# Counts in bf16 beside fp32 sums, biases in three bf16 parts, and ten register loads made one, in a one-core graph kernel

## The chip, the cores and the metric

The kernel runs on one core of a Trainium2 chip. The core has a matrix engine (PE, with its weight loads shown apart as PEld), a vector engine (DVE), an activation engine (ACT), GpSimd (POOL) and a queue engine for transfers (SP), each with an instruction stream of its own; semaphores tie them together. The metric is the device time of one execution in microseconds (us), as the median of several runs. One further execution was profiled, and the rows shown come from it.

## The reference

12,500 nodes with 128 features, 400,000 edges sorted by destination, each of one of two kinds. Cut to what matters:

```python
Xs = X[src]
m_data = Xs @ W_data.T + b_data
m_ctrl = Xs @ W_control.T + b_control
msg = jnp.where((edge_types == 0)[:, None], m_data, m_ctrl)
agg = jax.ops.segment_sum(msg, dst, num_segments=N)
h = relu(agg + (X @ W_self.T + b_self))
out = layernorm(X + h)            # no scale or shift
```

Since the sum is linear, the kernel sums the raw rows of `X` per destination and kind first, and multiplies by the weights once per node. The two edge biases then enter as a number of edges times a bias: a node with 20 edges of the first kind and 12 of the second gets 20 b_data + 12 b_control. That is what the counts are for.

## The kernel before, in words

**Groups and windows.** The edges are cut into 25 groups of 125 chunks of 128 edges; one group covers 500 destinations. In a group there are five windows, and in each window two kinds of work. In the first, whole rows of `x` (in three bf16 parts that add up to fp32) are gathered by indirect transfers on POOL (`msg`), a comparison on DVE makes a 0/1 matrix (`psel`) of which edge goes to which destination, and PE multiplies the two (L738). In the second, the rows are picked out of a copy of `x` held on the chip: DVE makes matrices `pick` and `esel`, PE picks rows (`got`, L893), ACT copies them to `emsg` (L907), and PE adds them up with `esel` (L738 again). A long chain of small DVE operations (`O`, `prod`, `found`, `rank`, `rm`, `rv`, `key`, `top`) works out where an edge goes, for a later pair of windows.

**Sums and counts.** Each window's sums land in PSUM (`sums`). `accumulate` (L782) adds them on DVE into `acc[g]`, an fp32 tile of 128 partitions by 3 planes by 640 destinations: planes 0 and 1 hold the sums for the two kinds, plane 2 the counts, kept in partitions 0 and 32 (a matmul with a matrix whose first column is ones, L824, makes them). A fixed 1 in partition 2 stands for the node's own bias. Where a window lies in the 640 columns is known only at run time: `place_of` (L776) reads that column number out of a small tile `place_i` into a DVE register, ten times in most groups (232 times in all), just ahead of the `accumulate` that uses it. Each read is three instructions on DVE's instruction stream: a TENSOR_LOAD, a FUSED_REGOPS and a SEQ_ASSERT that holds the value to its range. Every `accumulate` has one more FUSED_REGOPS, which makes the addresses.

**End of a group.** `pass_on` (L766) adds the last 140 columns of a group's `acc` to the next group's. `finish` then makes the output in four tiles of 125 nodes: per tile the fp32 matmuls of L1012 are x by W_self, the two planes of sums by their weights, and plane 2 by a matrix `bias` that has the three biases in rows 0, 32 and 2. Each fp32 matmul stands in the trace as two passes. Then come relu, the residual, the normalization and the store. `begin_acc` (L750) fills a new `acc` by a transfer from a stored start value.

**Order.** The program is written out in full, without loops at run time. The kernel's code gives a rough order by time fractions, and a scheduler then places the instructions on each engine; on DVE and on the other engines they run in that order. The register reads are kept behind an earlier `accumulate`. A second, slow path (`long_path`) runs only if one of the checks (`check_all`) finds that the edges don't fit the layout.

Of the kernel before, what the change touches and what calls it, by code (L numbers as in the profile page):

```python
# [8 lines left out]
FP = mybir.dt.float32  # L9
BF = mybir.dt.bfloat16  # L10
# [3 lines left out]
AF = mybir.ActivationFunctionType  # L14
OP = mybir.AluOpType
AX = mybir.AxisListType
# [3 lines left out]
P = 128  # L20
D = 128
# [4 lines left out]
NG = NC // GC  # L26
GN = P * GC * N // E
# [20 lines left out]
OVF = 64  # L48
TOP = 7
HOLD = 18  # L50
AHEAD = 14
# [154 lines left out]
def short_path(ctx, tc, const, ident, eps, wT, brow, bad, x, src, dst, etype, ws, bs, out):  # L206
    nc = tc.nc
# [32 lines left out]
    raw = {}  # L240
# [76 lines left out]
    tmp = early.enter_context(tc.tile_pool(name="tmp", bufs=1))  # L317
    wn = tmp.tile([P, 3, D], FP, name="wn")
    bias = keep.tile([P, D], FP, name="bias")
    nc.gpsimd.memset(bias, 0.0)  # L320
# [33 lines left out]


    start1 = keep.tile([P, 1], FP, name="start1")
    nc.vector.tensor_single_scalar(start1, lane_f, 2.0, op=OP.is_equal)
# [20 lines left out]
    nc.vector.memset(one_col[:, 0:1], 1.0)  # L378

    worst = keep.tile([P, 5, P], FP, name="worst")  # L380
    nc.vector.memset(worst, 0.0)
# [13 lines left out]
    def places_and_weights():  # L395
        place = tmp.tile([1, 2, NG, NWIN], FP, name="place")
        ref = tmp.tile([1, NG, NE, 2], I32, name="ref")
        nc.gpsimd.iota(ref, pattern=[[GN, NG], [0, NE], [-PAD, 2]], base=PAD - M0, channel_multiplier=0)
        ref = ref.rearrange("o g e k -> o g (e k)")
        for at, k in enumerate("pe"):  # L400
                each = place[:, 0].rearrange("o g (i k) -> o g i k", k=2)[:, :, :, at]
                nc.vector.tensor_tensor(
                    each, first_i[k], ref.rearrange("o g (i k) -> o g i k", k=2)[:, :, :, at], op=OP.subtract
                )
        nc.vector.tensor_tensor(place[:, 1], place[:, 0], least, op=OP.max)
        nc.vector.tensor_scalar(place[:, 1], place[:, 1], float(R - WMAX), None, op0=OP.min)
# [318 lines left out]
        return [(0.6, lambda: half(0, NCELL))]  # L725


    acc, added, parts_in = {}, [], {}

    def sums():  # L730
        return ps2.tile([P, 512], FP, name="sums")
# [9 lines left out]
        return last  # L741

    lap = R - GN
    acc_start = dram.tile([P, 3, R], FP, name="acc_start")

    def begin_acc(g):
        if g not in acc:
            acc[g] = fp.tile([P, 3, R], FP, name="acc")
            if g > 1:
                nc.sync.dma_start(out=acc[g], in_=acc_start)  # L750
                return
            at = lap if g else 0
            for cells, start in ((acc[g][:, 0:2, :], zero), (acc[g][:, 2, at:], start1), (acc[g][:, 2, :at], zero)):
                if cells.shape[-1]:
                    shape = list(cells.shape)
                    start = start.rearrange("p (o c) -> p o c", o=1) if len(shape) == 3 else start
                    nc.scalar.copy(cells, start.to_broadcast(shape))
            if g == 1:
                nc.sync.dma_start(out=acc_start, in_=acc[g])

    def pass_on(g):

        assert parts_in[g] == NE + sets(g)
        if g + 1 < NG:
            begin_acc(g + 1)
            added.append(nc.vector.tensor_add(acc[g + 1][:, :, :lap], acc[g + 1][:, :, :lap], acc[g][:, :, GN:]))  # L766

    def acc_rows(g, a, b):
        begin_acc(g)
        return acc[g][:, a:b, :]  # L770

    def place_of(g, i):

        parts_in[g] = parts_in.get(g, 0) + 1
        with tc.issue_after(added[-2].ins) if len(added) > 1 else ExitStack():
            return nc.vector.value_load(raw["place"][0:1, g, i:i + 1], min_val=0, max_val=R - WMAX)  # L776

    def accumulate(at, rows, ps, wide, width):

        n = rows.shape[1]  # L780
        win = rows[:, :, bass.ds(at, width)]
        added.append(nc.vector.tensor_add(win, win, ps[:, :n * wide].rearrange("p (a w) -> p a w", w=wide)[:, :, :width]))  # L782
# [46 lines left out]
    def gathered(g, i):  # L829
        n = of_p(g, i)  # L830
        s = {}

        def add_counts():
            s["at"] = place_of(g, 2 * i)
            accumulate(s["at"], acc_rows(g, 2, 3)[:2 * CAP], s["ps"][:2 * CAP, 2 * AW:], AW, AW)
# [24 lines left out]
        return evenly([lambda c=c: chunk(c) for c in range(n)])  # L860
# [122 lines left out]
    def finish_batch(g, tiles):  # L983
        s = {}
# [19 lines left out]
        def product(i):  # L1004
            if i == 0:
                s["ph"] = side()
            _, c, rows = tiles[i]
            terms = [(s["xT"][:, i * P:i * P + rows], wT[:, 2, :])]
            terms += [(acc[g][:, t, c:c + rows], wT[:, t, :]) for t in range(2)]
            terms += [(acc[g][:, 2, c:c + rows], bias)]  # L1010
            for j, (left, right) in enumerate(terms):
                nc.tensor.matmul(  # L1012
                    s["ph"][:rows, i * D:(i + 1) * D], left, right, start=(j == 0), stop=(j == len(terms) - 1)
                )
# [50 lines left out]

    def check_all():

        far = keep.tile([P, 7], FP, name="far")
# [9 lines left out]
        nc.vector.tensor_scalar(far[:, 6:7], far[:, 6:7], float(OVF), None, op0=OP.subtract)  # L1078
        nc.vector.tensor_single_scalar(far, far, 0.0, op=OP.is_gt)
        nc.tensor.transpose(pf[:7, 128:128 + P], far, ident)  # L1080
        most4 = keep.tile([7, 1], FP, name="most4")
        nc.vector.tensor_reduce(most4, pf[:7, 128:128 + P], AX.X, OP.max)
        nc.tensor.transpose(pf[:1, 256:263], most4, ident[:7, :7])
        one_i = keep.tile([1, 1], FP, name="one_i")
        nc.vector.tensor_reduce(one_i, pf[:1, 256:263], AX.X, OP.max)
        nc.vector.tensor_copy(bad, one_i)

    def begin_slots(w):
# [235 lines left out]
```

## Time and profile before

| | |
|---|---|
| median of 3 runs | 1736.49 us (1736.48 to 1737.98) |
| profiled execution | 1736.82 us, span 1735.1 us |
| PE busy (modelled ends) | 1585.6 us, 91% |
| DVE busy | 1559.6 us, 90% |
| ACT busy | 1228.9 us, 71% |
| POOL busy | 1243.4 us, 72% |

Busy times count data work alone: register instructions are not in them, and show only as idle time of their engine or as "DVEq" in the chain of work that ended last. The span is the profiled time from first to last instruction; the execution's own time is 1.7 us longer.

### The profile page before, as it was taken

Reading aid. Unit: us, or ns where it says so; the run is one execution under the profiler, and the core shown is the slowest. Engines: PE = TensorE matmul, PEld = TensorE weight load, DVE = VectorE, ACT = ScalarE, POOL = GpSimd, SP = SyncE. Lnnn points to the kernel's source line nnn. Section 1 sums busy time; section 2 is a strip of 40 time slices with the busy share of each in tenths; the row PEclk is TensorE's granted clock in tenths of the full one; section 3 lists DMA queues with packets and bytes.
Section 4 is the critical chain, followed back from the end, with each engine's and each line's share of the span. In section 5 each row is a group of like instructions: output and inputs, shape, how many; then the busy total and the mean of one; then the engine's idle time right before and its main releaser. Section 6 shows DMA issues by size and latency. Waiting matters only on the chain.

```text
span 1735.1 us, 67976 instructions
## 1 busy us (share of the span) xinstructions
PE 1585.6 (91%) x28250; PEld 1249.1 (72%) x28250; DVE 1559.6 (90%) x3642; ACT 1228.9 (71%) x2201; POOL 1243.4 (72%) x1059
## 2 busy tenths in 40 slices
PE   1699999999999999999999999999999999999997
PEld 0477777777677777777777777777777777777776
DVE  7898999999999999999898999899999898999983
ACT  5777777767777676767677777776777676777675
POOL 1276778877778776767787777776777777777671
PEclk9999999999999999999999999999999999999999
DMA  7844454555454454444545444544454544444441
GB/s 221 275 135 137 130 155 127 159 153 149 124 158 130 139 159 147 134 144 135 151 125 169 138 149 130 159 130 154 139 162 124 161 129 146 146 154 126 136 134 46
DMA packets 145646, 252.35 MB, mean 145 GB/s; under 512 B 35563, under 2 KB 111936, under 8 KB 145328
## 3 DMA queue, kind: packets, MB, share of 16 engines
q1 hardware_dynamic: 82670, 138.54, 23.6%
q0 software_dynamic: 50032, 102.98, 22.3%
q10 hardware_dynamic: 12626, 6.40, 1.3%
q8 instruction: 223, 3.65, 0.9%
q14 instruction: 95, 0.78, 0.1%
HBM read 230.17 MB, written 17.67 MB: 143 GB/s over the span
## 4 chain that ended last, share of the span: by engine, by line
DVE 43%; PE 39%; issue 9%; ACT 5%; DVEq 2%; DMA 2%; SPq 0%; ACTq 0%
PE sums L738 17%; PE got L893 13%; DVE esel L516 5%; DVE prod L622 4%; DVE pick L724 3%; DVE prod L617 3%; PE side L1012 3%; DVE rv L657 3%; DVE found L624 2%; DVE psel L516 2%; DVE prod L595 2%; DVE acc L782 2%; ACT emsg L907 2%; DVE O L516 2%; DVEq L776 2%
## 5 line engine op out<-in xcount | busy, mean ns | idle before, releaser
L793 POOL DMA_INDIRECT msg<-rows,idx_g x985 | 1174.3, 1192 | 361.6 <-issue 128.6
L907 ACT CAST emsg<-got 128x768 bf16<-128x768 f32 (+1 forms) x1070 | 953.7, 931 | 360.1 <-PE got L893 338.4
L738 PE MATMUL sums<-esel,emsg 128*128 128x176 bf16 x7704 | 686.6, 240 | 0.6 <-ACT emsg L907 0.4
L738 PEld LDWEIGHTS <-emsg 128*128 128x128 bf16 x7704 | 566.0, 98 | 102.8 <-issue 95.5
L893 PE MATMUL got<-x,pick 128*32 128x384 bf16 x10486 | 584.8, 330 | 15.2 <-DVE pick L724 9.7
L893 PEld LDWEIGHTS <-pick 128*32 128x32 bf16 x10486 | 239.7, 96 | 135.0 <-DVE pick L724 12.1
L516 DVE TENSOR_TENSOR esel<-code_col,code 128x1760 bf16<-128x1760 bf16 x321 | 293.0, 913 | 16.2 <-PE sums L738 14.9
L738 PE MATMUL sums<-psel,msg 128*128 128x48 bf16 x2955 | 183.6, 184 | 31.3 <-DVE acc L782 29.3
L738 PEld LDWEIGHTS <-msg 128*128 128x128 bf16 x2955 | 153.8, 97 | 62.4 <-issue 58.3
L622 DVE TENSOR_TENSOR prod<-prod 128x1200 bf16<-128x1200 bf16 x214 | 133.7, 625 | 4.7
L516 DVE TENSOR_TENSOR O<-cell_col,blk 128x2000 bf16<-128x2000 bf16 x107 | 127.6, 1193 | 8.2 <-ACT blk L420 3.7
L617 DVE TENSOR_TENSOR prod<-O,ahead 128x2000 bf16<-128x2000 bf16 x107 | 128.4, 1200 | 5.8 <-DVE ahead L613 3.5
L782 DVE TENSOR_TENSOR acc<-acc,sums 128x80 f32 (+3 forms) x357 | 98.9, 280 | 32.4 <-PE sums L738 29.8
L516 DVE TENSOR_TENSOR psel<-near_col,near 128x1200 bf16<-128x1200 bf16 x125 | 97.4, 779 | 23.1 <-issue 22.4
L724 DVE TENSOR_SCALAR pick<-pick,lane_f 128x3200 bf16<-128x3200 bf16 x107 | 112.8, 1054 | 0.6 <-DMA pick<-there 0.6
L868 POOL DMA_INDIRECT both<-rows,idx x54 | 63.4, 1174 | 64.6 <-ACT emsg L907 27.0
L669 PE MATMUL side<-rv,O 128*128 128x64 bf16 x2140 | 83.6, 195 | 23.0 <-DVE rv L657 21.5
L669 PEld LDWEIGHTS <-O 128*128 128x128 bf16 x2140 | 78.8, 100 | 24.9 <-DVE rv L657 21.8
L657 DVE TENSOR_TENSOR rv<-rm,vals 128x1280 bf16<-128x1280 bf16 x107 | 87.8, 820 | 0.0
L624 DVE TENSOR_REDUCE found<-prod 128x20 f32<-128x600 bf16 x107 | 83.0, 776 | 5.2 <-DVE prod L622 2.7
L595 DVE TENSOR_TENSOR prod<-O 128x1000 bf16<-128x1000 bf16 x107 | 71.8, 671 | 0.0
L605 PEld LDWEIGHTS <-ltri 128*128 128x128 bf16 x1284 | 40.4, 97 | 36.3 <-issue 34.5
(171 smaller groups left out, 1536.2 us busy)
## 6 DMA issues: line engine op xcount, KB each, us to landing
pick<-there SPq DMA_DIRECT2D x106, 800.0 KB
acc<-acc_start SPq DMA_DIRECT2D x23, 960.0 KB
msg<-rows,idx_g POOLq DMA_INDIRECT x985
rows<-x SPq DMA_DIRECT2D x6, 1344.0 KB
xs<-in_x_dram SPq DMA_DIRECT2D x99, 62.5 KB
out_dram<-h SPq DMA_DIRECT2D x99, 62.5 KB
xt<-in_x_dram ACTq DMA_DIRECT2D x6, 896.0 KB
there<-cell SPq DMA_DIRECT2D x106, 6.2 KB
```

The source lines that it names most:

```text
L516: nc.vector.tensor_tensor(sel.rearrange("p n (w t) -> p n w t", t=2), col[:rows].rearrange("p (o w t) -> p o w t", o=1, t=2).to_broadcast( ...
L617: nc.vector.tensor_tensor(prod[:, :, :NCELL], s["O"], ahead.rearrange("p (o j) -> p o j", o=1).to_broadcast([P, EC, NCELL]), op=OP.mult,)
L622: nc.vector.tensor_add(prod[:, :, :h], prod[:, :, :h], prod[:, :, h:2 * h])
L624: nc.vector.tensor_reduce(found, prod[:, :, :h], AX.X, OP.add)
L657: placed[:] = [nc.vector.tensor_tensor(rv.rearrange("p c v (r t) -> p c v r t", t=2), rm.rearrange("p c (o r t) -> p c o r t", o=1, t=2).t ...
L669: nc.tensor.matmul(s["rk"][:m, :2 * CAP], s["held"][:, c * NCELL:c * NCELL + m], s["rv"][:, c].rearrange("p v r -> p (v r)"), start=(c == ...
L724: nc.vector.tensor_scalar(t, t, lane_f, None, op0=OP.is_equal)
L738: last = nc.tensor.matmul(out, msg[:, j * D:(j + 1) * D], sel, start=(start and j == 0), stop=stop, skip_group_check=True)
L782: added.append(nc.vector.tensor_add(win, win, ps[:, :n * wide].rearrange("p (a w) -> p a w", w=wide)[:, :, :width]))
L793: return nc.gpsimd.indirect_dma_start(out=msg, out_offset=None, in_=rows3[:, :], in_offset=bass.IndirectOffsetOnAxis(ap=codes["p", g][0][: ...
L893: last = nc.tensor.matmul(ps[CAP * a:CAP * (a + 1), :], slots[w]["pick"][:, a * NQ + q, :], x3[:, 4 * q + a - a0].rearrange("p j d -> p (j ...
L907: s["out"] = nc.scalar.copy(msg[:, :n], ps[:, :n, :3 * D])
```

## The change

The counts leave `acc` and get a tile of their own, `cnt[g]`, 128 by 640 in bf16 (fp32 in the last group). Whole numbers up to 256 are exact in bf16. The biases are split into three bf16 parts that add up to the fp32 value, and lie in rows 0 to 2, 32 to 34 and 3 to 5 of `bias_b`; the ones matrix of L824 has three columns of ones, so that a count stands in three partitions. With both sides in bf16, the bias matmul of a tile is one pass in place of two; the last group keeps fp32. Since a count over 255 would not be exact, ACT sums relu(count - 255.5) over each finished `cnt` (one instruction a group, in `pass_on`), and `check_all` sends the program to the slow path where that is over zero. The start values and `pass_on`'s addition are now two each, one for the sums and one for the counts. Some small DVE operations at the start split the biases.

The places of a group are now read by one TENSOR_LOAD into ten registers at the group's first `accumulate`, with no range check on DVE.

```diff
-        at = (0, CAP, 2)[i]
-        nc.sync.dma_start(out=bias[at:at + 1, :], in_=row)
+        at = (0, CAP, PARTS)[i]
+        nc.sync.dma_start(out=bias[at:at + PARTS, :], in_=row.to_broadcast([PARTS, D]))
...
+        later = tmp.tile([P, 2], FP, name="later")
+        for k in range(PARTS - 1):
+            nc.vector.tensor_reduce(later[:, k:k + 1], ident[:, k + 1::PARTS], AX.X, OP.add)
+        nc.vector.tensor_scalar(later, later, -1.0, None, op0=OP.mult)
+        nc.vector.tensor_tensor(later[:, 0:1], later[:, 0:1], later[:, 1:2], op=OP.add)
+        for k in range(PARTS - 1):
+            nc.vector.tensor_copy(bias_b, bias)
+            nc.vector.scalar_tensor_tensor(bias, bias_b, later[:, k:k + 1], bias, op0=OP.mult, op1=OP.add)
+        nc.vector.tensor_copy(bias_b, bias)
+        nc.vector.tensor_copy(bias, bias_b)
...
-            acc[g] = fp.tile([P, 3, R], FP, name="acc")
+            acc[g] = fp.tile([P, 2, R], FP, name="acc")
+            cnt[g] = fp.tile([P, R], BF, name="cnt") if g < NG - 1 else keep.tile([P, R], FP, name="cnt_last")
             if g > 1:
                 nc.sync.dma_start(out=acc[g], in_=acc_start)
+                if g < NG - 1:
+                    nc.sync.dma_start(out=cnt[g], in_=cnt_start)
...
-            added.append(nc.vector.tensor_add(acc[g + 1][:, :, :lap], acc[g + 1][:, :, :lap], acc[g][:, :, GN:]))
+            nc.vector.tensor_add(acc[g + 1][:, :, :lap], acc[g + 1][:, :, :lap], acc[g][:, :, GN:])
+            added.append(nc.vector.tensor_add(cnt[g + 1][:, :lap], cnt[g + 1][:, :lap], cnt[g][:, GN:]))
+            spill = fp.tile([P, R], BF, name="spill", bufs=1)
+            nc.scalar.activation(
+                spill[:2 * CAP], cnt[g][:2 * CAP], AF.Relu, bias=most[:2 * CAP], accum_out=over_c[:2 * CAP, g:g + 1]
+            )
...
-        with tc.issue_after(added[-2].ins) if len(added) > 1 else ExitStack():
-            return nc.vector.value_load(raw["place"][0:1, g, i:i + 1], min_val=0, max_val=R - WMAX)
+        if g not in at_places:
+            with tc.issue_after(added[-2].ins) if len(added) > 1 else ExitStack():
+                _, at_places[g] = nc.values_load_multi_w_load_instructions(
+                    raw["place"][0:1, g, :], engines=[nc.vector.engine], min_val=0, max_val=R - WMAX,
+                    skip_runtime_bounds_check_because="places are held to this range by a max and a min on the chip",
+                )
+        return at_places[g][i]
...
-            terms += [(acc[g][:, 2, c:c + rows], bias)]
+            terms += [(cnt[g][:, c:c + rows], bias_b if g < NG - 1 else bias)]
```

How the instructions stand. On DVE, near the start of the third group, before (L776 the register reads, L782 `accumulate`):

```order
L782 TENSOR_TENSOR acc<-acc,sums 64x120
L776 TENSOR_LOAD place_i
L776 ISA x2
L516 TENSOR_TENSOR O<-cell_col_142,blk_3030 128x2000
L782 ISA
L782 TENSOR_TENSOR acc<-acc,sums 128x2x88
L516 TENSOR_TENSOR esel<-code_col,code 128x1584
L776 TENSOR_LOAD place_i
L776 ISA x2
L613 TENSOR_REDUCE ahead<-side 128x100
L776 TENSOR_LOAD place_i
L776 ISA x2
```

The same place with the change (L807 is the read, L817 `accumulate`, L792 the counts' part of `pass_on`):

```order
L639 TENSOR_TENSOR prod<-prod 128x20x60
L533 TENSOR_TENSOR psel<-near_col,near_2424 128x1200
L639 TENSOR_TENSOR prod<-prod 128x20x30
L641 TENSOR_REDUCE found<-prod 128x20
L807 TENSOR_LOAD place_i
L817 ISA
L817 TENSOR_TENSOR cnt<-cnt,sums 64x120
L643 CAST rank<-found 128x40
L792 TENSOR_TENSOR cnt<-cnt 128x140
L533 TENSOR_TENSOR rm<-rank_col,rank 128x640
```

The reads with their two register instructions are gone from between the data operations; one read of ten stands right ahead of the group's first `accumulate`.

A later group's start on DVE with the change, where a short operation stands ahead of the read:

```order
L741 TENSOR_SCALAR pick<-pick,lane_f 128x3200
L651 MAX top<-key 128x8
L807 TENSOR_LOAD place_i
L817 ISA
L817 TENSOR_TENSOR cnt<-cnt,sums 64x120
L656 TENSOR_SCALAR full<-top 128x16
L660 CAST top_i<-top 128x16
L533 TENSOR_TENSOR esel<-code_col,code 128x1760
```

Of the 25 reads in the program with the change, six stand behind a MAX, six behind `O`, three behind `found`, three behind `om_all`, and seven behind other operations. Past the opening part the scheduler's order on DVE differs from before in most places by a few instructions.

On PE, one output tile of `finish` among the picking matmuls, before:

```order
L893 MATMUL got_4711<-x_114,pick 32x384
L1012 MATMUL side<-wT,xT 125x128
L1012 MATMUL side<-wT,acc 125x128 x2
L1012 MATMUL side<-bias,acc 125x128
L893 LDWEIGHTS pick
```

and with the change:

```order
L930 MATMUL got_4604<-x_114,pick 32x384
L1049 MATMUL side<-wT,xT 125x128
L1049 MATMUL side<-wT,acc 125x128 x2
L1049 LDWEIGHTS cnt
L1049 MATMUL side<-bias_b,cnt 125x128
L930 LDWEIGHTS pick
```

The bias term of a tile became a bf16 weight load and matmul; it stands where it stood. An fp32 matmul's weight load has no row of its own in such a list.

More of the change, by code (lines that the diff above doesn't have):

```diff
@@ L48 @@
 OVF = 64
+PARTS = 3
 TOP = 7
@@ L319, in short_path @@
     bias = keep.tile([P, D], FP, name="bias")
+    bias_b = keep.tile([P, D], BF, name="bias_b")
     nc.gpsimd.memset(bias, 0.0)
@@ L356, in short_path @@
     start1 = keep.tile([P, 1], FP, name="start1")
-    nc.vector.tensor_single_scalar(start1, lane_f, 2.0, op=OP.is_equal)
+    nc.vector.tensor_reduce(start1, ident[:, PARTS:2 * PARTS], AX.X, OP.add)
+    over_c = keep.tile([P, NG], FP, name="over_c")
+    nc.gpsimd.memset(over_c, 0.0)
+    most = keep.tile([P, 1], FP, name="most")
+    nc.gpsimd.memset(most, 0.5 - 256.0)
     blks = [keep.tile([P, NE, 2 * EC], BF, name=f"blk{k}") for k in range(3)]
@@ L725, in pick_matrix @@
         return [(0.6, lambda: half(0, NCELL))]
-    acc, added, parts_in = {}, [], {}
+    acc, added, parts_in, at_places = {}, [], {}, {}
     def sums():
@@ L743, in short_path @@
     lap = R - GN
-    acc_start = dram.tile([P, 3, R], FP, name="acc_start")
+    acc_start = dram.tile([P, 2, R], FP, name="acc_start")
+    cnt_start = dram.tile([P, R], BF, name="cnt_start")
+    cnt = {}
     def begin_acc(g):
         if g not in acc:
-            acc[g] = fp.tile([P, 3, R], FP, name="acc")
+            acc[g] = fp.tile([P, 2, R], FP, name="acc")
+            cnt[g] = fp.tile([P, R], BF, name="cnt") if g < NG - 1 else keep.tile([P, R], FP, name="cnt_last")
             if g > 1:
                 nc.sync.dma_start(out=acc[g], in_=acc_start)
+                if g < NG - 1:
+                    nc.sync.dma_start(out=cnt[g], in_=cnt_start)
+                else:
+                    nc.scalar.copy(cnt[g][:, lap:], start1.to_broadcast([P, GN]))
+                    nc.scalar.copy(cnt[g][:, :lap], zero.to_broadcast([P, lap]))
                 return
             at = lap if g else 0
[L753 to L757, printed above, removed]
+            nc.scalar.copy(acc[g], zero.rearrange("p (o c) -> p o c", o=1).to_broadcast([P, 2, R]))
+            nc.scalar.copy(cnt[g][:, at:], start1.to_broadcast([P, R - at]))
+            if at:
+                nc.scalar.copy(cnt[g][:, :at], zero.to_broadcast([P, at]))
             if g == 1:
                 nc.sync.dma_start(out=acc_start, in_=acc[g])
+                nc.sync.dma_start(out=cnt_start, in_=cnt[g])
     def pass_on(g):
@@ L834, in add_counts @@
             s["at"] = place_of(g, 2 * i)
-            accumulate(s["at"], acc_rows(g, 2, 3)[:2 * CAP], s["ps"][:2 * CAP, 2 * AW:], AW, AW)
+            begin_acc(g)
+            rows = cnt[g][:2 * CAP].rearrange("p (o r) -> p o r", o=1)
+            accumulate(s["at"], rows, s["ps"][:2 * CAP, 2 * AW:], AW, AW)
         def chunk(c):
@@ L1066, in check_all @@
     def check_all():
-        far = keep.tile([P, 7], FP, name="far")
+        far = keep.tile([P, 8], FP, name="far")
         nc.vector.tensor_reduce(far[:, :5], worst, AX.X, OP.max)
@@ L1078, in check_all @@
         nc.vector.tensor_scalar(far[:, 6:7], far[:, 6:7], float(OVF), None, op0=OP.subtract)
+        nc.vector.tensor_reduce(far[:, 7:8], over_c, AX.X, OP.max)
         nc.vector.tensor_single_scalar(far, far, 0.0, op=OP.is_gt)
[L1080 to L1083, printed above, removed]
+        nc.tensor.transpose(pf[:8, 128:128 + P], far, ident)
+        most4 = keep.tile([8, 1], FP, name="most4")
+        nc.vector.tensor_reduce(most4, pf[:8, 128:128 + P], AX.X, OP.max)
+        nc.tensor.transpose(pf[:1, 256:264], most4, ident[:8, :8])
         one_i = keep.tile([1, 1], FP, name="one_i")
-        nc.vector.tensor_reduce(one_i, pf[:1, 256:263], AX.X, OP.max)
+        nc.vector.tensor_reduce(one_i, pf[:1, 256:264], AX.X, OP.max)
         nc.vector.tensor_copy(bad, one_i)
```

2 lines of the change are left out of this document (1 added, 1 removed).

## The prediction

> **What bounds the kernel now.** I read the page's engine table first, then the windows view for a stretch in the middle, the chain of work that ended last, and the waits.
>
> ```profile
> PE 1585.6 (91%) x28250; PEld 1249.1 (72%) x28250; DVE 1559.6 (90%) x3642; ACT 1228.9 (71%) x2201; POOL 1243.4 (72%) x1059
> core 0: us, PE busy (x) PEld busy (x) DVE busy (x) ACT busy (x) POOL busy (x), PEclk, DMA share, GB/s
> 1000.00:1500.00 500.00, 472.89 (x8497) 374.44 (x8494) 460.01 (x1069) 356.32 (x656) 377.10 (x318) 1.00 0.47 145
> DVE 43%; PE 39%; issue 9%; ACT 5%; DVEq 2%; DMA 2%; SPq 0%; ACTq 0%
> PE sums L738 17%; PE got L893 13%; DVE esel L516 5%; DVE prod L622 4%; DVE pick L724 3%; DVE prod L617 3%; PE side L1012 3%; DVE rv L657 3%; DVE found L624 2%; DVE psel L516 2%; DVE prod L595 2%; DVE acc L782 2%; ACT emsg L907 2%; DVE O L516 2%; DVEq L776 2%
> ```
>
> In the middle stretch PE is busy 473 of 500 us, DVE 460, ACT 356, at the full clock (1.00). No engine bounds the kernel alone: the chain goes 43% over DVE and 39% over PE, changing sides every few microseconds. ACT, POOL and the transfers are hardly on it. So time taken from either engine counts by about the share in which the chain lies on it, not in full.
>
> ```profile
> DVE acc L782 <- PE sums L738: 29.8, 51, 1.3
> DVE psel L516 <- issue: 22.4, 43, 1.5
> PE sums L738 <- DVE acc L782: 29.5, 53, 1.5
> DVE x L293 <- issue: 2.5, 1, 2.5
> DVE parts L494 <- issue: 2.3, 5, 0.5
> DVE O L516 <- issue: 2.2, 4, 0.7
> ACT emsg L907 <- PE got L893: 338.4, 431, 4.2
> ```
>
> The columns are us in total, times, longest. The two engines wait for each other by the same amount (29.8 and 29.5 us). DVE's second largest wait is for nothing: 22.4 us ahead of `psel` and 7.0 us in the three smaller rows are "issue". ACT waits 338 us for PE, so it has room.
>
> **What DVE's empty waits are.** The view of the source line L776, and a piece of the chain (start, us, what) where two reads follow each other:
>
> ```profile
> L776 DVEq TENSOR_LOAD <-place_i x232: 296/304/1402, 42.1 to 1721.3; - x116
> L776 DVEq FUSED_REGOPS  x232: 183/190/206, 43.4 to 1721.7; - x116
> L776 DVEq SEQ_ASSERT  x232: 23/23/31, 43.6 to 1721.9; - x116
> ...
> 837.41 0.12 DVE acc L782
> 837.54 0.09 DVEq L776
> ...
> 838.05 0.31 DVEq L776
> 838.36 0.08 issue
> 838.44 0.19 DVEq L776
> ...
> 838.69 0.05 issue
> 838.73 0.78 DVE psel L516
> ```
>
> Each read takes 0.30 + 0.19 + 0.02 us and some gaps, 0.68 us from 838.05 to 838.73, and no data operation starts meanwhile. What runs on DVE ahead of it covers it: here nothing does, and DVE stands from 837.54 to 838.73. Elsewhere a long operation hides it.
>
> **The reads that go.** On the chain, DVEq L776 is 2% of 1735.1, 35 us, between 26 and 43 by rounding. The waits with "issue" sum to 22.4 + 2.5 + 2.3 + 2.2 = 29.4. I take **-29 us**, with 43 as the far end. Near end: where the read goes, PE's sums may be late next (the 29.8 us row), so that only half, 15, comes back.
>
> **The read that comes.** 25 of them, each ten registers. The trace has no read of more than one register. Bounds: 0.30 us (a read costs what a read costs) and 10 x 0.304 = 3.04 us (ten reads in a row). What covers it is the operation ahead of it on DVE, by the order shown above:
>
> ```profile
> L634 DVE MAX8 top<-key 128x8 f32<-128x20 f32 x107 | 18.2, 171 | 0.6
> L516 DVE TENSOR_TENSOR O<-cell_col,blk 128x2000 bf16<-128x2000 bf16 x107 | 127.6, 1193 | 8.2 <-ACT blk L420 3.7 <-issue 2.2 <-ACT emsg L907 1.2
> L624 DVE TENSOR_REDUCE found<-prod 128x20 f32<-128x600 bf16 x107 | 83.0, 776 | 5.2 <-DVE prod L622 2.7
> L541 DVE TENSOR_SCALAR om_all<-slot_col,side 128x448 bf16<-128x448 bf16 x107 | 42.9, 440 | 1.0 <-PE side L535 0.5
> L766 DVE TENSOR_TENSOR acc<-acc 128x420 f32<-128x420 f32 x24 | 14.2, 590 | 0.2
> ```
>
> Six stand behind 0.17 us, six behind 1.19, three behind 0.78, three behind 0.44, and seven behind others that I take at 0.4: cover 14.6 us in all. To the read I add 0.2 us for the gaps and `accumulate`'s own address step. At 0.30 the exposed time is 6 x 0.33 + 3 x 0.06 + 7 x 0.1 = 3 us. At 3.04 it is 25 x 3.24 - 14.6 = 66 us. Between ends ten apart I take their geometric middle as an estimate, 1.0 us a read, since no row shows whether the 0.30 us go with the instruction or with the register: 6 x 1.03 + 3 x 0.42 + 3 x 0.76 + 7 x 0.8 = **+15 us**. Behind it in DVE's stream is the group's first `accumulate`, and with it the `sums` buffer that PE wants back (the 29.5 us row).
>
> The Trainium skill ("Runtime: NRT & Kernel Launch", Instruction fetch mechanics) states some 200 ns a register for such loads from HBM, even in bulk. By it, as an estimate, the read takes 2.0 us and exposes 25 x 2.2 - 14.6 = 40 us, which would turn the sum. The trace's 304 ns for one register, from on-chip memory, neither confirms nor rules it out.
>
> **The bias matmul.** PE's timeline shows one output tile, then bf16 work, and the page the mean length of the latter:
>
> ```profile
> 827.62 0.49 PE L1012 MATMUL side<-wT,xT 128*125 128x128 f32 x2
> 827.95 0.60 PE L1012 MATMUL side<-wT,acc 128*125 128x128 f32 x4
> 828.38 0.38 PE L1012 MATMUL side<-bias,acc 128*125 128x128 f32 x2
> 829.13 1.31 PE L738 MATMUL sums<-esel,emsg 128*128 128x176 bf16 x15
> L738 PE MATMUL sums<-esel,emsg 128*128 128x176 bf16 x7704 | 686.6, 240 | 0.6 <-ACT emsg L907 0.4
> L1012 PE MATMUL side<-bias,acc 128*125 128x128 f32 (+2 forms) x202 | 38.6, 273 | 0.0
> ```
>
> Four passes start between 827.95 and 828.38, so a pass takes 0.108 us, and a bias term two: 0.215. A bf16 matmul of 176 columns comes every (1.31 - 0.24) / 14 = 0.076 us, and 128 columns will not take longer. Saved: 0.139 us in 96 of the 101 tiles (202 passes; the last group's five stay), 13.3 us of PE. L1012 has 808 passes, 87 us, and 3% of the span, 52 us, on the chain: a share of 0.6 (0.5 to 0.7). So **-8 us**.
>
> A weight load could spoil this:
>
> ```profile
> L669 PEld LDWEIGHTS <-O 128*100 128x100 bf16 x107 | 13.6, 127 | 0.0
> L605 PEld LDWEIGHTS <-ltri 128*128 128x128 bf16 x1284 | 40.4, 97 | 36.3 <-issue 34.5 <-PE sums L738 0.5
> ```
>
> 100 columns take longer (127 ns) than 128 (97); here there are 125. If that load isn't hidden behind matmuls the saving falls to 0.215 - 0.127 = 0.09 us a tile, and the term to -5. The Trainium skill ("TensorE: Matmul & The Clock Gate", Weight-path perf modes) has this as a rule: the fast load works only with exactly 128 weights that aren't fp32; the two rows agree. By its plain rate (P / 1.2 ns) the estimate is 104 ns a tile, and a term of -6 in place of -8.
>
> **What else is added.** Nearest rows for ACT's test on 64x640:
>
> ```profile
> L757 ACT COPY acc<-start 128x640 f32<-128x640 f32 x1 | 0.7, 737 | 0.0
> L1042 ACT ACTIVATE h<-h,nm,rs 125x128 f32<-125x128 f32 x99 | 40.9, 485 | 3.8 <-DVE nm L1038 3.6
> L1002 ACT COPY xT<-side 128x125 f32<-128x125 f32 x99 | 19.1, 280 | 13.0 <-PE side L1000 12.9
> ```
>
> A 640-column copy takes 0.74 us; an ACTIVATE with operands takes 0.2 more than a copy. So 0.9 us, 24 times, 22 us of ACT. Queued behind it are the `emsg` copies, on which PE waits. ACT's 338 us of waiting is the cover, and ACT's share of the chain is 5% for 71% busy: 0.07 of 22, so **+2 us**; with no cover, 22. `pass_on` becomes two additions, two thirds of 0.59 and a short one of 0.17 (as MAX) to 0.37: 0.56 to 0.76 us for 0.59, at most 4 us, **+1**. Some ten small operations at the start split the biases, about 2 us of DVE, half of it on the chain, **+1**; the 2.5 us wait ahead of `x` L293, two cold reads, is in the 29. The counts' own additions read PSUM as before: 0. SP's queue gets one more transfer behind each refill of `acc`, of a tile that is free when `acc` is; the refill shrinks by a third, and SP is not on the chain: 0, unless a `pick` transfer stands behind it.
>
> **The sum.** The profiled execution took 1736.8 us (span 1735.1 and 1.7 around it), 0.3 above the median. 1736.8 - 29 + 15 - 8 + 2 + 1 + 1 = 1718.8; less 0.3 for the median, **1718 us**. By the unknown terms' bounds this case runs from 1705 to 1733.
>
> **Rivals.**
> 1. *Ten reads in series.* The registers are fetched one after the other and the DVE stream stands at each group's start, with `sums` held and PE behind it. It turns the sign where exposed time passes 29 + 8 - 4 = 33 us, at a read of 1.7 us. At 2.3 us, the middle between that and 3.04: 25 x 2.5 - 14.6 = 48, so 1718 + 33 = 1751 us; at 3.04, 1769. For it: the registers' instructions are slow throughout (0.19 us for a few steps). Against: none of the rows shows a price per register. The skill's 2.0 us would give 1743. Chance 0.22.
> 2. *A read costs what a read costs.* 0.30 us, exposed 3: 1706 us, with the full 35 us of the chain 1700. For it: one instruction, ten neighbouring words. Chance 0.18.
> 3. *PE is the bound.* DVE's regained time returns as waiting for `sums` (the 29.8 us row grows), and only the matmuls' -8 and the additions' +4 stay: 1732 to 1736. For it: PE 473 of 500. Against: 43% of the chain on DVE. Chance 0.10.
> 4. *The test stops ACT at a bad place.* Each of the 24 delays an `emsg` that PE needs next: +20, 1738 us. Chance 0.08.
>
> The slow path is no rival: nodes have 32 edges on average, and no count comes near 255.
>
> **How the numbers follow.** 0.42 is left for the forecast. About 0.2%, 3.5 us, is what a measurement of this kernel can tell. Faster by more: 0.39 of the forecast, all of rival 2, half of 3, some 0.01 of rival 1: 0.63. Slower by more: nearly all of rival 1 and a part of 4: 0.24. Within: 0.13. The range 1698 to 1748 leaves out the upper half of rival 1 and a little below.
>
> **What would show it.** Right: 25 TENSOR_LOADs at about 1 us; "issue" ahead of `psel` near zero; a new idle time on the groups' first `accumulate` near 15 us in all; bias passes 96 + 10 in place of 202; the test near 0.9 us with no new wait of PE for `emsg`. Wrong: loads of 2 us and more; or loads short and the waits of `acc` for PE's sums grown by what was gained; or a PE wait at the test.

## The result: 1742.2 us, 0.33% slower

| | before | changed |
|---|---|---|
| median | 1736.54 us (1735.38 to 1737.98, 9 runs) | 1742.23 us (1739.36 to 1746.84, 9 runs) |
| profiled execution | 1736.82 us, span 1735.1 | 1746.84 us, span 1745.0 |
| PE, DVE, ACT busy | 1585.6, 1559.6, 1228.9 us | 1588.9, 1555.4, 1249.5 us |

The ratio is 1.0033, 95% interval 1.0021 to 1.0045. The sign of the forecast (1718 us, faster) is wrong; the time lies inside the range. The profiled execution of the changed kernel is the slowest of its nine, 4.6 us over their median, so its waits are a little long.

The page of the changed kernel, from the engine table, the chain and the groups (the line numbers have moved: L533 was L516, L755 was L738, L817 was L782, L807 was L776):

```profile
PE 1588.9 (91%) x28154; PEld 1238.1 (71%) x28154; DVE 1555.4 (89%) x3677; ACT 1249.5 (72%) x2251; POOL 1266.2 (73%) x1061
PE 43%; DVE 41%; issue 8%; ACT 4%; DMA 3%; DVEq 0%; SPq 0%; POOL 0%; ACTq 0%; POOLq 0%
L533 DVE TENSOR_TENSOR psel<-near_col,near 128x1200 bf16<-128x1200 bf16 x125 | 96.1, 769 | 0.0
L533 DVE TENSOR_TENSOR esel<-code_col,code 128x1760 bf16<-128x1760 bf16 x321 | 293.2, 913 | 20.4 <-PE sums L755 19.0
L817 DVE TENSOR_TENSOR acc<-acc,sums 128x176 f32 (+2 forms) x232 | 66.5, 289 | 58.2 <-PE sums L755 49.2
```

By the page the register reads have left the chain (DVEq from 2% to 0%), and the idle time ahead of `psel`, 22.4 us by "issue" before, is 0.0. What was freed came back in other rows: `acc` now waits 49.2 us for PE's sums (29.8 before) and `esel` 19.0 (14.9 before). The waits view shows both engines' side, first DVE's rows and then one of PE's:

```profile
DVE acc L817 <- PE sums L755: 49.2, 62, 3.4
DVE cnt L817 <- issue: 5.6, 6, 2.2
DVE acc L817 <- issue: 2.9, 2, 2.4
PE sums L755 <- DVE cnt L817: 35.8, 46, 1.9
```

"issue" is 5.6 + 2.9 us where the four rows before had 29.4. That isn't all that the ten-register reads expose, since the profile puts a wait down to the semaphore that came last. The read of a group and the `accumulate` behind it:

```profile
L807 DVEq TENSOR_LOAD <-place_i x1: 2295/2295/2295, 1341.5 to 1341.5; - x1
1344.05 0.34 DVE L817 TENSOR_TENSOR acc<-acc,sums 128x176 f32 x1 [1.81 <-PE got L930]
```

The idle time is put down to PE, but it ends about 0.27 us behind the end of the read. Of the 25 first `accumulate`s of a group, 13 start so, 0.19 to 0.27 us behind their read, after 20.0 us of idle time in all. PE waits 35.8 us for DVE where it waited 29.5.

The rows of the changed operations themselves, by source line (durations min/median/max in ns):

```profile
L807 DVEq TENSOR_LOAD <-place_i x25: 1062/1316/2317, 75.2 to 1671.3; - x25
L1049 PEld LDWEIGHTS <-cnt x96: 116/136/137, 149.7 to 1712.3; 128*125 128x125 bf16 x95, 128*75 128x75 bf16 x1
L1049 PE MATMUL side<-bias_b,cnt x96: 219/219/249, 149.8 to 1712.4; 128*125 128x128 bf16 x95, 128*75 128x128 bf16 x1
L794 ACT ACTIVATE spill<-cnt,most x24: 827/828/832, 134.0 to 1658.3; 64x640 bf16<-64x640 bf16 x24
L794 ACT ACTIVATION_READ_ACCUMULATOR spill<-cnt,most x24: 185/187/195, 134.8 to 1659.1; 64x1 f32 x24
L791 DVE TENSOR_TENSOR acc<-acc x24: 432/438/451, 146.2 to 1701.8; 128x280 f32<-128x280 f32 x24
L792 DVE TENSOR_TENSOR cnt<-cnt x23: 205/218/283, 143.7 to 1624.2; 128x140 bf16<-128x140 bf16 x23
```

The bias passes, the test and the additions measure close to what the prediction took. The read doesn't have one duration: taken one by one, it takes about 1.06 us in the even groups (the very first 1.32) and about 2.30 us in the odd ones. A group's row of ten words is 40 bytes, so even groups begin at a multiple of 16 bytes and odd ones 8 bytes past one, counted from the start of the tile.

### The profile page after: what moved, and what is told of

The parts are those of the page before. It is cut to its first block, busy times and chain, and to the rows that moved or that the text cites. A ratio compares the mean times of both kernels' runs of the same rounds, so it can differ in the third digit from the quotient of the medians.

```text
span 1745.0 us, 67260 instructions
## 1 busy us (share of the span) xinstructions
PE 1588.9 (91%) x28154; PEld 1238.1 (71%) x28154; DVE 1555.4 (89%) x3677; ACT 1249.5 (72%) x2251; POOL 1266.2 (73%) x1061
## 4 chain that ended last, share of the span: by engine, by line
PE 43%; DVE 41%; issue 8%; ACT 4%; DMA 3%; DVEq 0%; SPq 0%; POOL 0%; ACTq 0%; POOLq 0%
PE sums L755 19%; PE got L930 14%; DVE esel L533 5%; DVE prod L639 4%; PE side L1049 4%; DVE pick L741 4%; DVE rv L674 3%; DVE found L641 3%; DVE prod L634 3%; DVE prod L612 2%; DVE psel L533 2%; ACT emsg L944 2%; DVE rm L533 2%; PE side L622 2%; DVE O L533 1%
## 5 line engine op out<-in xcount | busy, mean ns | idle before, releaser
L828 POOL DMA_INDIRECT msg<-rows,idx_g x985 | 1194.3, 1213 | 349.0 <-issue 134.4
L755 PE MATMUL sums<-esel,emsg 128*128 128x176 bf16 x7704 | 693.6, 240 | 2.2 <-DVE acc L817 1.9
L755 PEld LDWEIGHTS <-emsg 128*128 128x128 bf16 x7704 | 566.8, 98 | 111.6 <-issue 104.2
L930 PE MATMUL got<-x,pick 128*32 128x384 bf16 x10486 | 591.9, 331 | 17.8 <-DVE pick L741 10.6
L533 DVE TENSOR_TENSOR esel<-code_col,code 128x1760 bf16<-128x1760 bf16 x321 | 293.2, 913 | 20.4 <-PE sums L755 19.0
L755 PE MATMUL sums<-psel,msg 128*128 128x48 bf16 x2955 | 184.3, 184 | 39.8 <-DVE cnt L817 35.8
L755 PEld LDWEIGHTS <-msg 128*128 128x128 bf16 x2955 | 152.6, 97 | 72.9 <-issue 69.4
L533 DVE TENSOR_TENSOR O<-cell_col,blk 128x2000 bf16<-128x2000 bf16 x107 | 127.3, 1189 | 0.5 <-ACT blk L437 0.5
L817 DVE TENSOR_TENSOR acc<-acc,sums 128x176 f32 (+2 forms) x232 | 66.5, 289 | 58.2 <-PE sums L755 49.2
L533 DVE TENSOR_TENSOR psel<-near_col,near 128x1200 bf16<-128x1200 bf16 x125 | 96.1, 769 | 0.0
L630 DVE TENSOR_REDUCE ahead<-side 128x100 bf16<-128x200 f32 x107 | 38.8, 363 | 32.8 <-PE side L622 29.5
```

Of the source, the lines that this page charges most:

```text
L533: nc.vector.tensor_tensor(sel.rearrange("p n (w t) -> p n w t", t=2), col[:rows].rearrange("p (o w t) -> p o w t", o=1, t=2).to_broadcast( ...
L755: last = nc.tensor.matmul(out, msg[:, j * D:(j + 1) * D], sel, start=(start and j == 0), stop=stop, skip_group_check=True)
L828: return nc.gpsimd.indirect_dma_start(out=msg, out_offset=None, in_=rows3[:, :], in_offset=bass.IndirectOffsetOnAxis(ap=codes["p", g][0][: ...
L930: last = nc.tensor.matmul(ps[CAP * a:CAP * (a + 1), :], slots[w]["pick"][:, a * NQ + q, :], x3[:, 4 * q + a - a0].rearrange("p j d -> p (j ...
```

## Experiments

Three theories were held against each other from here.

- **A, the read.** The 2.30 us reads stall DVE, PE runs dry behind them and then gets a halved clock; this eats the gain.
- **B, the order.** The scheduler places the whole program anew when the single reads are gone, and the new order makes DVE and PE wait for each other more.
- **C, the test.** ACT's test of the counts holds up the `emsg` copies, and PE with them.

Beside them stands the prediction's third rival, "PE is the bound": freed DVE time turns into waiting for sums, whatever the order.

### One part of the change at a time

All reads but the first at 1.06 us (`aligned`; its order on every engine is that of the changed kernel):

```diff
-        place_i = raw["place"] = keep.tile([1, NG, NWIN], I32, name="place_i")
-        nc.vector.tensor_copy(place_i, place[:, 1])
+        place_i = raw["place"] = keep.tile([1, NG, NWIN + 2], I32, name="place_i")
+        nc.vector.tensor_copy(place_i[:, :, :NWIN], place[:, 1])
...
-                    raw["place"][0:1, g, :], engines=[nc.vector.engine], min_val=0, max_val=R - WMAX,
+                    raw["place"][0:1, g, :NWIN], engines=[nc.vector.engine], min_val=0, max_val=R - WMAX,
```

> The changed kernel with one difference: each group's row of place_i is 12 words long in place of 10, so that every row starts at a multiple of 16 bytes; the instructions stand in the same order on every engine. In the changed kernel's trace the reads of ten took 1.06 us at groups 2, 4, ... and 2.30 us at groups 1, 3, .... Theory A (a long read stands DVE, PE idles behind it, and its clock is then halved for 3.4 us): all 25 reads near 1.06 us, the exposed time of reads falls from 12.8 us to about 4, half-clock stretches in the middle of the span become rarer, and the time falls by 4 to 8 us against the changed kernel, to 1734 to 1738. Theory B (the order in which the engines wait for each other sets the pace, and stalls of DVE are absorbed): reads get shorter as well, but the time stays within 2 us of the changed kernel's 1742. Theory C (the test on ACT holds PE): no change, 1742.

Measured 1738.32 us (1734.26 to 1742.19, 11 runs), ratio to before 1.0003 (0.9993 to 1.0014). The edit does what it says:

```profile
L807 DVEq TENSOR_LOAD <-place_i x25: 1060/1065/1324, 76.4 to 1665.3; - x25
```

In this order the long reads are worth some 4 us, 1742.2 to 1738.3, of the 24 that the result lies above the forecast. That is about the least that theory A expected and more than theory B did, so this run doesn't decide between them. The idle time behind the reads, taken as above, falls by 12.8 us, from 20.0 to 7.2, so most of it doesn't come through.

Without the test (`no_test`), which leaves a count over 255 unnoticed:

```diff
-            spill = fp.tile([P, R], BF, name="spill", bufs=1)
-            nc.scalar.activation(
-                spill[:2 * CAP], cnt[g][:2 * CAP], AF.Relu, bias=most[:2 * CAP], accum_out=over_c[:2 * CAP, g:g + 1]
-            )
```

> The changed kernel without ACT's test of the counts (24 ACTIVATE with a sum over 64x640, L794): left out is the detection of a count over 255, so the flag for the slow path lacks that part. The order on DVE is the same, on PE and ACT nearly. Theory A (long reads and the halved clock): no change beyond 2 us, 1741. Theory B (order): no change beyond 2 us. Theory C (the test holds PE, 24 x 1.0 us of ACT, of which up to half is on the path): 5 to 12 us faster, 1730 to 1737.

Measured 1740.05 us (1736.71 to 1742.19, 11 runs), ratio 1.0016 (1.0007 to 1.0025): 2 us, the +2 of the prediction, though the interval overlaps that of the changed kernel. Theory C, which expected 5 to 12 us, falls.

The ten-register read alone on the kernel before (`reads_only`), with fp32 counts and the two-pass bias:

```diff
-        with tc.issue_after(added[-2].ins) if len(added) > 1 else ExitStack():
-            return nc.vector.value_load(raw["place"][0:1, g, i:i + 1], min_val=0, max_val=R - WMAX)
+        if g not in at_places:
+            with tc.issue_after(added[-2].ins) if len(added) > 1 else ExitStack():
+                _, at_places[g] = nc.values_load_multi_w_load_instructions(
+                    raw["place"][0:1, g, :], engines=[nc.vector.engine], min_val=0, max_val=R - WMAX,
+                    skip_runtime_bounds_check_because="places are held to this range by a max and a min on the chip",
+                )
+        return at_places[g][i]
```

> The kernel before with the reads alone changed: ten registers by one TENSOR_LOAD a group, no range check; counts stay fp32 in acc. Theory A: it gains the 29 us of register waits on DVE less about 13 us of exposed reads less some 5 us of halved clock, times a share of about a half: 1728 to 1733. Theory B (the order sets the pace, and freed DVE time returns as waiting for PE's sums): within 4 us of 1736.5, with the wait of acc for sums grown by 15 us or more. Theory C (the test): as the prediction, 1725 to 1730, since there is no test here.

Measured 1753.99 us (1753.33 to 1754.8, 4 runs), ratio 1.0098 (1.0083 to 1.0114). The part that was to bring 14 us costs 17. None of the three theories had this time. Theory B's sign is there, a wait of `acc` for PE's sums of 53.4 us (29.8 before), but B had expected no change in the time.

The change without that part (`counts_only`: the changed kernel with the `place_of` of before, the same diff the other way round):

> The changed kernel with the reads as before (one value at a time, with the range check); counts in bf16, biases in parts, and the test are in. Theory A: PE saves 16 us of matmul spacing, ACT gets 24 us; 1726 to 1732, and no half-clock stretch beyond those before. Theory B: within 4 us of 1736.5. Theory C (the test holds PE): the saving is eaten by the test, 1736 to 1745.

Measured 1733.17 us (1730.54 to 1736.43, 11 runs), ratio 0.9976 (0.9965 to 0.9987): 3.7 us faster than before, where the prediction's terms for this part sum to -8 + 2 + 1 + 1 = -4. Theory B's range has this time, those of A and C miss it by 1 and 3 us. So the trouble sits in the reads' part; A and B are left for it.

### The order held fast

The scheduler can be made to keep a given order: for two instructions that are to follow each other on an engine, the later one gets an edge to the earlier. The edge binds the scheduler alone and puts no semaphore into the program. The order is that of the data instructions of another kernel of this study, kept as a packed table for each engine; register instructions stay where the scheduler puts them. The traces bear it out: in the four runs with all orders held, PE and DVE run their data instructions in the sequence of the kernel that the order is from, but for a few of some 28,000 and 3,700, and the number of semaphore instructions on each engine is that kernel's too.

```diff
+    keep_order(tc, ORDER)
...
+        for a, b in zip(row, row[1:]):
+            tc.add_manual_dep(
+                b, a.name, mybir.DependencyInfo(mybir.DependencyClass.NoSync, mybir.DependencyReason.DATA), reason="order"
+            )
```

With it, read and order can be crossed. First the reads alone (as `reads_only`, with rows of 12 words, so that all reads but the first take 1.06 us) in the order of the kernel before:

> The kernel before with only the ten-register read, rows of 12 words so that every read takes 1.06 us, and every data instruction of all five engines held in the order that the kernel before has. reads_only, the same edit in the scheduler's new order, took 1754.0 us. Order: if the new order is what costs, the reads' own term comes out here: 29 us of empty waits go and some 10 us of exposed long reads come, so 1712 to 1728. Read: if the long read and the halved clock after it cost it, the same as reads_only less the 4 us that alignment gave, 1745 to 1752. PE bound: if DVE's freed time only turns into waits for PE's sums whatever the order, 1733 to 1738.

Measured 1725.12 us (1724.19 to 1727.02, 6 runs), ratio 0.9926 (0.9913 to 0.9939): 12.4 us faster than the 1737.49 beside it. The prediction had -29 + 15 = -14 for it.

Then the counterpart, the kernel before, with its single reads, in the order of `reads_only`:

> The kernel before with its single reads (232 of 0.30 us) and fp32 counts, but with the data instructions of all five engines held in the order of reads_only. Nothing is left of the change but the order. Order: this order is bad by itself and the short reads come on top: 1750 to 1775, with DVE's waits of acc for PE's sums near 50 us. Read: the order is as good as the old one, 1735 to 1739, and the waits of acc for sums stay near 30 us. PE bound: 1737 to 1745, since DVE's extra 29 us were hidden behind the waits for PE.

Measured 1772.73 us (1766.26 to 1775.59, 5 runs), ratio 1.0185 (1.0166 to 1.0203). Its groups and its chain:

```profile
DVE 40%; PE 39%; issue 9%; ACT 6%; DMA 3%; DVEq 2%; POOL 1%; SPq 0%; ACTq 0%; POOLq 0%
L542 DVE TENSOR_TENSOR esel<-code_col,code 128x1760 bf16<-128x1760 bf16 x321 | 293.4, 914 | 25.1 <-PE sums L764 23.4
L808 DVE TENSOR_TENSOR acc<-acc,sums 128x80 f32 (+3 forms) x357 | 99.2, 279 | 52.3 <-PE sums L764 51.0
L542 DVE TENSOR_TENSOR psel<-near_col,near 128x1200 bf16<-128x1200 bf16 x125 | 97.2, 777 | 27.1 <-issue 26.6
```

Here is no ten-register read, no bf16 count and no test; only the order differs from the kernel before. It costs 35 us by itself, and it brings the wait of `acc` for PE's sums that the changed kernel shows (51.0; before 29.8). The empty waits ahead of `psel` stay, 26.6 us, since the single reads do. Theory B's prediction held in both; theory A said 1745 to 1752 for the first and 1735 to 1739 for the second, and "PE is the bound" 1733 to 1738 and 1737 to 1745.

Now the whole change in the order of `counts_only`, with rows of 12 words (`all_pinned`) and with the reads as they are (`after_pinned`):

> The whole change with rows of 12 words (all reads 1.06 us), every data instruction held in the order of counts_only, which has the change without the ten-register read and took 1733.2 us. The aligned change in its own order took 1738.3. Order: 1733.2 less what the short reads expose there (29 us) plus some 10 us for the long ones, 1708 to 1724, and the wait of acc for sums falls back from 53 to between 25 and 40 us. Read: 1736 to 1741, as in its own order. PE bound: 1729 to 1734.

> The changed kernel as it is (rows of ten words, so every second read takes 2.30 us), every data instruction held in the order of counts_only. Beside all_pinned it shows what the longer odd reads cost in a good order; beside the changed kernel what the order costs. Order: 1712 to 1730, 4 to 12 us over all_pinned (12 reads longer by 1.24 us are 15 us, part of them under the operation ahead). Read: 1740 to 1745, as the changed kernel. PE bound: 1729 to 1735, within 2 us of all_pinned.

`all_pinned`: 1714.7 us (1712.42 to 1716.72, 4 runs), ratio 0.9861 (0.9844 to 0.9878). `after_pinned`: 1727.58 us (1726.23 to 1728.99, 6 runs), ratio 0.9939 (0.9926 to 0.9952). The second is the changed kernel itself, data instruction for data instruction, in another order; it is 14.7 us faster than the changed kernel, and faster than before. The odd reads cost 12.9 us between the two, a little over the 4 to 12 expected. The groups of `after_pinned`:

```profile
L559 DVE TENSOR_TENSOR esel<-code_col,code 128x1760 bf16<-128x1760 bf16 x321 | 292.6, 912 | 14.2 <-PE sums L781 13.2
L843 DVE TENSOR_TENSOR acc<-acc,sums 128x176 f32 (+2 forms) x232 | 66.6, 289 | 44.5 <-PE sums L781 34.9
```

Against the changed kernel, idle time ahead of `esel` falls from 20.4 to 14.2 and ahead of `acc` from 58.2 to 44.5: 19.9 us together, and the two spans differ by 19.3 (1745.0 and 1725.7; the medians by 14.7).

**One such place.** The changed kernel's DVE timeline (start, us, operation), then PE's, around one `accumulate`:

```profile
1003.59 1.20 DVE L634 TENSOR_TENSOR prod<-O,ahead 128x2000 bf16<-128x2000 bf16 x1
1004.83 0.78 DVE L639 TENSOR_TENSOR prod<-prod 128x1200 bf16<-128x1200 bf16 x1
1006.73 0.40 DVE L817 TENSOR_TENSOR acc<-acc,sums 128x240 f32 x1 [1.12 <-PE sums L755]
1007.05 0.47 DVE L639 TENSOR_TENSOR prod<-prod 128x600 bf16<-128x600 bf16 x1
...
1005.31 1.31 PE L755 MATMUL sums<-esel,emsg 128*128 128x176 bf16 x15
1006.46 0.24 PE L755 MATMUL sums<-psel,msg 128*128 128x48 bf16 x3
```

The same `accumulate` in `after_pinned`:

```profile
990.70 1.20 DVE L660 TENSOR_TENSOR prod<-O,ahead 128x2000 bf16<-128x2000 bf16 x1
991.93 1.29 DVE L665 TENSOR_TENSOR prod<-prod 128x1200 bf16<-128x1200 bf16 x2
993.26 0.78 DVE L667 TENSOR_REDUCE found<-prod 128x20 f32<-128x600 bf16 x1
994.07 0.18 DVE L669 CAST rank<-found 128x40 bf16<-128x40 f32 x1
994.29 0.49 DVE L559 TENSOR_TENSOR rm<-rank_col,rank 128x640 bf16<-128x640 bf16 x1
994.70 0.40 DVE L843 TENSOR_TENSOR acc<-acc,sums 128x240 f32 x1
...
992.41 1.31 PE L781 MATMUL sums<-esel,emsg 128*128 128x176 bf16 x15
993.56 0.24 PE L781 MATMUL sums<-psel,msg 128*128 128x48 bf16 x3
```

PE does the same in both. In the changed kernel `accumulate` stands between the halves of `prod`, and DVE idles 1.12 us until the sums are there, with `prod`'s second half, `found`, `rank` and `rm` queued behind it. In the other order they run first, and the wait is gone. This place comes back with the groups: the `accumulate` at 135.75, 397.82, 1006.73, 1269.67 and 1536.71 us of the changed kernel idles 1.1 to 1.2 us behind `prod`, and in the other order 0.0 to 0.15. That makes some 5.5 of the 19.9 us; the other places weren't taken one by one.

### Which engine's order

As `all_pinned`, but only DVE's order held, or only PE's, or only those of ACT, POOL and SP; the scheduler places the rest around them.

> As all_pinned (the whole change, all reads 1.06 us), but only DVE's order is held to that of counts_only; the scheduler places PE, ACT and the queues around it. All five held gave 1714.7, none 1738.3. If it is DVE's order that costs: 1712 to 1720, and the wait of acc for PE's sums stays near 39 us. If it is PE's order: 1730 to 1740, acc for sums near 50. If both must fit each other: between, 1720 to 1730.

> As all_pinned, but only PE's order is held to that of counts_only, and the scheduler places DVE and the rest around it. If it is DVE's order that costs: 1730 to 1740. If it is PE's order: 1712 to 1720. If both must fit each other: 1720 to 1730, or worse than 1738, since an order made for one engine holds up the other.

> As all_pinned, but only the orders of ACT, POOL and SP are held to those of counts_only; DVE's and PE's come from the scheduler. If DVE's or PE's order costs: 1732 to 1745, like the aligned change in its own order (1738.3). If ACT's or the queues' order were the cause: 1712 to 1720.

| orders held | time (us) | ratio to before |
|---|---|---|
| none (`aligned`) | 1738.32 | 1.0003 (0.9993 to 1.0014) |
| ACT, POOL, SP | 1745.83 (1743.74 to 1747.06) | 1.0048 (1.0035 to 1.0060) |
| PE | 1770.19 (1764.26 to 1771.95) | 1.0188 (1.0172 to 1.0203) |
| DVE | 1725.30 (1723.99 to 1727.91) | 0.9937 (0.9925 to 0.9949) |
| all five | 1714.70 (1712.42 to 1716.72) | 0.9861 (0.9844 to 0.9878) |

DVE's order alone brings 13.0 of the 23.6 us. PE's alone makes it worse by 32; that the scheduler then makes a bad order for DVE around it fits, but wasn't tested. The orders of ACT, POOL and SP alone make it worse by 7.5, a little outside the 1732 to 1745 expected; they weren't what cost the time. The waits with one engine's order held:

```profile
DVE acc L839 <- PE sums L777: 35.6, 61, 1.3
DVE esel L555 <- PE sums L777: 14.3, 27, 1.6
```

with DVE's order held, and with PE's alone

```profile
DVE acc L839 <- PE sums L777: 60.8, 75, 2.4
DVE esel L555 <- PE sums L777: 29.9, 35, 2.9
```

The expectation "If both must fit each other" is what came: 1720 to 1730 for DVE's order alone, worse than 1738 for PE's. The same instructions span 55 us with nothing but their order changed.

## Why the prediction was wrong, by its steps

The ladder from before to the changed kernel, each rung one run:

| step | us | difference |
|---|---|---|
| before | 1736.5 | |
| counts, bias matmul, test (`counts_only`) | 1733.2 | -3.4 |
| ten-register reads, all short, same order (`all_pinned`) | 1714.7 | -18.5 |
| odd rows at 2.30 us, same order (`after_pinned`) | 1727.6 | +12.9 |
| the scheduler's own order (changed kernel) | 1742.2 | +14.7 |

`counts_only` has an order of its own too, so its rung holds the parts and that order together (beside its own runs of before it was 3.7). The runs of before beside each of the others have medians of 1736.5 to 1737.5.

- **The reads that go, -29, and the read that comes, +15.** Together -14; measured -12.4 in the order of before and -18.5 in that of `counts_only`. The net is near, but in part by luck. The short reads exposed less than the 15 taken, 5.5 us in `reads_pinned` and 6.9 in `all_pinned` (idle time that ends within 0.3 us behind the read), and part of what was freed came back as waiting. Of DVE's idle time, 33 us lie under register instructions before and 4 in `reads_pinned`, so some 30 went and 12.4 came through. DVE waits longer for PE's sums in both than in the kernel whose order it is, where it was 29.8 us (before) and 25.5 (`counts_only`). The rows of `reads_pinned`, then `all_pinned`:

```profile
DVE acc L813 <- PE sums L764: 41.7, 66, 3.4
DVE acc L843 <- PE sums L781: 38.7, 61, 4.8
```

  As it ran, the read was mis-sized in every second group: 2.30 us, 12.9 us more in the held order. In the scheduler's order this is only 4 us, 1742.2 to 1738.3; why it counts for less there was not shown.
- **Ten reads in series (rival 1).** Its price, 2.3 us, is that of the odd groups, but not its mechanism: ten words at 1.06 us are no series of ten times 0.304. What was to show the sum right, "near 15 us" of new idle time on the groups' first `accumulate`, came as 20.0 us, of which some 8 stand under "issue". The Trainium skill's 200 ns a register for loads from HBM ("Runtime: NRT & Kernel Launch", Instruction fetch mechanics) stands between the two prices measured here from on-chip memory, 106 and 230 ns a register.
- **The bias matmul, -8.** On PE, the time from each bias term's first pass to the instruction behind it sums to some 26 us before and 10 after: 16 us, where 13.3 were taken. With ACT and additions the part came out within 1 us of its -4, in an order of its own that wasn't held.
- **The test, +2; the additions, +1.** 0.83 and 0.19 us on ACT; 2 us by `no_test`, at the edge of what the runs can tell. On DVE 0.44 + 0.22 = 0.66 for 0.59 us.
- **The step that failed** is the sum. It took every other wait of the two engines from the trace of before and changed only the terms it named. The chain and its shares, from which it judged what an engine's time is worth, are those of one order. The section on the change had said that the order on DVE "differs from before in most places by a few instructions", and the prediction gave that no term. It was the largest after the reads themselves: 14.7 us in the changed kernel, 23.6 with all reads short, 35 in the kernel before. That 1742 us lies inside the range is luck: the range went that high for long reads in series and for the test, not for the order.
- **PE is the bound (rival 3)** foretold the sign that would be seen, the `acc` row growing by what was gained, and a time 6 to 10 us short of the result. But it isn't the whole: in the held orders 12.4 and 18.5 us did come through, with PE 92% busy. In part it was right, since the wait of `acc` for PE's sums grew there too, by 12 and 13 us.

**What stays open.** Why the scheduler's rules come to a worse order when the reads go was not tried. The 10.6 us between holding DVE's order and holding all five weren't divided further. That 16 bytes are what decides the read's price fits every read except the first of each run, but other row lengths than 40 and 48 bytes weren't run.

## What to carry to other kernels

Where a scheduler orders the program, an edit is two edits: the instructions it changes, and the order of all the others. Cross them, by running the edit in the old order and the old instructions in the new order, before judging either; a good edit can be thrown away by a worse order. And when two engines hand work to each other all the time, look at what stands directly behind a waiting instruction: if it is independent work, try it ahead of the wait, as in the place shown.

## What the hardware showed

- **A read of ten registers** from on-chip memory took 1.06 us where the row begins at a multiple of 16 bytes in its tile and 2.30 us where it begins 8 bytes past one; a single register took 0.30 us. Rows of 12 words made all reads but the first short; the first took 1.3 to 2.4 us.
- **PE's clock halved around some short idles.** PE's timeline in the changed kernel, behind an idle of 1.81 us, the windows view of that stretch (the last columns are the granted clock, the DMA share and GB/s), and the end of the same idle in `aligned`, with its stretch:

```profile
1355.52 0.23 PE L755 MATMUL sums<-psel,msg 128*128 128x48 bf16 x3 [1.81 <-DVE cnt L817]
...
1357.32 2.38 PE L755 MATMUL sums<-esel,emsg 128*128 128x176 bf16 x15
...
1361.67 1.30 PE L755 MATMUL sums<-esel,emsg 128*128 128x176 bf16 x15
1350.00:1364.00 14.00, 11.93 (x203) 9.69 (x200) 12.22 (x23) 7.93 (x15) 11.10 (x10) 0.88 0.42 125
...
1354.60 0.23 PE L755 MATMUL sums<-psel,msg 128*128 128x48 bf16 x3 [1.60 <-DVE cnt L817]
1347.00:1361.00 14.00, 12.40 (x248) 10.56 (x250) 13.74 (x27) 9.46 (x15) 11.26 (x10) 1.00 0.50 151
```

In the changed kernel fifteen matmuls took 2.38 us, then 1.30 again. The granted clock was 0.5 for 3.4 us there, at two more places around idles of 1.86 and 2.71 us, and for 6.8 us around one of 4.83 at the start; before had no such stretch between 70 and 1729 us. The long reads aren't what made the three idles in the middle, as theory A has it: with short reads PE idles at the same places, for 1.60, 1.86 and 3.21 us in `aligned`. Nor does the length of an idle alone decide: in `aligned` the clock fell at the 3.21 us, and stayed full at the 1.60 and the 1.86. The Trainium skill ("TensorE: Matmul & The Clock Gate", What's actually happening) gives the gate a window of about 3.4 us: the length of the slow stretches agrees, but the clock fell around idles half as long. It isn't the cause of the result: `order_only` had six such stretches without any long read, `after_pinned` three and is 14.7 us faster. At half the clock a stretch can cost at most half its length, 8.5 us in all in the changed kernel and 5.1 in `after_pinned`.
